# First image of an attention and cluster kernel: the second block's first keys kept in SBUF, its queries taken from SBUF, the maximum spread one value pair sooner

## The chip, the cores and the metric

The kernel runs on one core of a Trainium2 chip. TensorE multiplies matrices (its weight loads are listed apart from its matmuls), VectorE (DVE) and ScalarE (ACT) work on SBUF and PSUM, GpSimd (POOL) works on SBUF, and SyncE (SP) issues most of the DMAs. The metric is the device time of one execution in microseconds, as the median of several runs.

## The reference

Four images of 256 channels and 64 x 64 pixels pass two layers. The first is self-attention over the 4096 pixels of an image:

```python
q = jnp.einsum('oc,bcn->bno', wq, xf) + bq            # 32 channels
k = jnp.einsum('oc,bcn->bon', wk, xf) + bk[None, :, None]
attn = jax.nn.softmax(jnp.einsum('bnd,bdm->bnm', q, k), axis=-1)
v = jnp.einsum('oc,bcn->bon', wv, xf) + bv[None, :, None]
out = jnp.einsum('bcn,bmn->bcm', v, attn).reshape(B, Cc, H, W)
return gamma[0] * out + x
```

The second layer, which the change doesn't touch, is a group norm, a clustering of the pixels, an MLP with GELU, and a pointwise convolution, all over the same images.

## The kernel before, in words

**Tiles and units.** An image's 4096 queries are cut into 8 blocks of 512, and its 4096 keys into 8 groups of 512. A unit is one group against one block, so an image has 64 units, numbered block by block: unit 8 is the second block's first unit and takes key group 0 again. Each unit has two halves of 256 keys. `products` (L484) makes a half's scores in a PSUM tile `sc`, `kept` (L501) copies them on ACT into the unit's slot `s` in SBUF, and `highest_of` (L506) takes the running maximum `top` on DVE. In `half` (L521) the copy comes first and the maximum reads the same PSUM tile after it. The maximum of a block is folded (`fold`, L566), turned over by four transposes (`turned_over`, tile `tt`), reduced and put on a diagonal `dg` (`across`, L578), and spread over all partitions by one matrix product into the PSUM tile `hold` (`spread`, L640). `exps` (L649) subtracts it from the scores on DVE and takes the exponentials on ACT; `factors` (L666) adds pieces on DVE and POOL; `weigh` (L716) multiplies them with the values into the accumulators `av`.

**Keys and queries.** Both have 32 channels, cut into a high and a low part and stacked four times along the partitions, so that one product of 128 partitions multiplies all pairs of parts. `projected` (L346) projects four blocks at a time into 128 partitions; `halves_of` (L359) splits the result. There are two ways to the stacked form. `straight` (L381) moves one block with four DMAs of 64 KB from SBUF to SBUF, one for each part, each from 32 partitions to every fourth partition. Or `written` (L376) first writes the split rows to DRAM with four DMAs of 256 KB (on POOL's queue here), and `q_block` (L458) or `k_unit` (L463) loads a stacked block back with one DMA of 256 KB on SP, which waits for the writes.

**The first image's start** is `alone` (L865), an order written out by hand; the program keeps it on every engine. `staged` (L393) projects blocks 0 to 3 of keys and queries into one tile `st` and makes the stacked keys of groups 0 to 3 and the queries of block 0 straight from it. Groups 4 to 7 are made straight from the tile `hl_k`, with 16 DMAs on SP that are issued after unit 0. While the 8 units of block 0 are scored, the values are projected pair by pair (`v_pair`, L453: eight matmuls, then an eviction on ACT), and POOL writes the split rows to DRAM after units 2 to 5. After unit 3 the queries of block 1 and the keys of unit 8 are loaded back from DRAM; the keys of unit 9 are loaded when unit 8 begins (`begun`, L469). Behind these loads on SP's queue come the weights `mix`, `fvb`, `wproj` and the smaller parameters (`load_rest`, L176). After the last unit come the fold, `v_pair(11)`, the transposes, unit 8's first half, `v_pair(12)`, `across`, `v_pair(13)`, `spread`, `v_pair(14)`, and `wf` (L283: four small matmuls and two copies on ACT); then `exps(0)`.

**Buffers.** Keys in the stacked form for units 0 and 1 and for 8 onward take two buffers (tag `k`) in turn; queries take two (tag `q`). The pool `spool` has 13 buffers of 8 KB a partition, given to tiles as they come: four tiles of the image, `st`, three sums, and the slots of units 0 to 4 fill it. Slots 5 and 6 take the buffers of the first two image tiles. The third and fourth image tiles are still read by `v_pair(8)` to `v_pair(15)`, so the slot of unit 7 takes the buffer of `st`: in the program's memory map, the two have the same address. Its first write, ACT's copy of unit 7's first half, therefore waits for all DMAs that read `st`.

Of the kernel before, what the change touches and what calls it, by code (L numbers as in the profile page):

```python
# [9 lines left out]
F32R = mybir.dt.float32r  # L10
# [4 lines left out]
P = 128  # L15
# [3 lines left out]
NB = 512  # L19
# [10 lines left out]
RG, GRP = 4, N // NB  # L30
# [30 lines left out]
def attention_then_cluster_block(  # L61
# [26 lines left out]
    work = ctx.enter_context(tc.tile_pool(name="work", bufs=2))  # L88
# [87 lines left out]
    def load_rest():  # L176
        load_mix("first")
        yield
        nc.sync.dma_start(out=fvb[:, ED:], in_=v_b.partition_broadcast(P))
        nc.sync.dma_start(out=wproj_s[:ED], in_=wproj)  # L180
        nc.sync.dma_start(out=wproj_s[ED:, :], in_=pc[:, ipb : ipb + 1].rearrange("c o -> o c"))
        yield
        for i, f in enumerate(behind):
            f()
            if i == 2:
                yield
        yield
        nc.gpsimd.tensor_tensor(pw_q[1], pw_q[1], pw_q[3], ALU.add)
        nc.gpsimd.tensor_scalar(pw_q[3], pw_q[3], -1.0, None, ALU.mult)
        yield  # L190
# [63 lines left out]
    def roots():  # L254
        for s, v in ((dw_d, "dw_v"), (pw_s, "pw_v")):
            rsqrt(s, par(v), BN_EPS)
        table(AF.Exp)
# [80 lines left out]
    def attention(b, xs, ys):  # L338
# [5 lines left out]
        qs, ks, slots, mxs, accs, tops, rdens, ts = {}, {}, {}, {}, {}, {}, {}, {}  # L344
# [28 lines left out]
        def part_of(which, c, hi, lo):  # L373
            return (hi if c in ((0, 2) if which == "k" else (0, 1)) else lo).bitcast(F32)
# [6 lines left out]
        def straight(which, r, dst, hi, lo, other=nc.sync):  # L381
            for c in range(4):
                (other if c % 2 else nc.sync).dma_start(
                    out=dst[c::4].bitcast(F32),
                    in_=part_of(which, c, hi, lo)[r * D : (r + 1) * D],
                )

        def stacked(which, nb):

            i, r = divmod(nb, RG)  # L390
            return own[which][i, r * D : (r + 1) * D].rearrange("d c n -> (d c) n")

        def staged():  # L393

            st = spool.tile([P, 4, NB], F32R, tag="s", name=f"st_{b}")
            ps = ps_s.tile([P, 2, NB], F32, tag="s", name=f"pr_{b}")
            k0, q0 = (st[:, 0], st[:, 1]), (st[:, 2], st[:, 3])
            for j, w in enumerate("kq"):  # L400
                projected(w, 0, ps[:, j])
            halves_of("k", *k0, ps[:, 0])
            k_straight(0, k0)
            qs[0] = work.tile([P, NB], F32R, tag="q", name=f"q_{b}_0")
            halves_of("q", *q0, ps[:, 1])
            straight("q", 0, qs[0], *q0, nc.scalar)
            for u in range(1, 4):
                k_straight(u, k0)
            return k0, q0
# [27 lines left out]
        def v_step(i, k):  # L437
            if i == k == 0:
                own["v"] = big.tile([P, N // P, C], F32, tag="v", name=f"v_{b}")
            if i % 2 == k == 0:  # L440
                vps[0] = ps_m.tile([P, 2, C], F32, tag="m", name=f"vp_{b}_{i // 2}")
            o = (i * P) % XT
            nc.tensor.matmul(  # L443
                vps[0][:, i % 2, :],
                xs[i * P // XT][:, k, o : o + P],
                wv_s[:, k, :],
                start=(k == 0),
                stop=(k == KC - 1),
            )
            if i % 2 and k == KC - 1:  # L450
                nc.scalar.copy(own["v"][:, i - 1 : i + 1, :], vps[0])

        def v_pair(i):  # L453
            for j in range(2 * i, 2 * i + 2):
                for k in range(KC):
                    v_step(j, k)

        def q_block(nb):  # L458

            qs[nb] = work.tile([P, NB], F32R, tag="q", name=f"q_{b}_{nb}")  # L460
            nc.sync.dma_start(out=qs[nb].bitcast(F32), in_=stacked("q", nb))

        def k_unit(u):  # L463

            g = u % GRP
            ks[u] = big.tile([P, NB], F32R, tag="k", bufs=2, name=f"k_{b}_{u}")
            nc.sync.dma_start(out=ks[u].bitcast(F32), in_=stacked("k", g))
# [30 lines left out]
        def tiles(t):  # L498
            return t.rearrange("p r (h n) -> p r h n", h=2)

        def kept(u, h, sc):  # L501
            nc.scalar.copy(slots[u][:, PAIR[h]].rearrange("p h r n -> p r h n"), tiles(sc))  # L502
# [69 lines left out]
        def turned_over(nb, tp):  # L572
            top = tops.pop(nb)
            for j in range(4):
                nc.tensor.transpose(tp[:, j, :], top[:, 0, j * P : (j + 1) * P], ident)
            return tp

        def across(nb, tag="w2", tp=None):  # L578
            if tp is None:
                tp = turned_over(nb, ps_m.tile([P, 4, P], F32, tag="m", name=f"tt_{b}_{nb}"))  # L580
            mx = small.tile([P, 4], F32, tag="mx", name=f"mx_{b}_{nb}")
            nc.vector.tensor_reduce(mx, tp, AX.X, ALU.max)
            dg = work.tile([P, 4, P], F32, tag=tag, bufs=1, name=f"dg_{b}_{nb}")
            nc.vector.tensor_tensor(
                dg,
                ident.unsqueeze(1).to_broadcast([P, 4, P]),
                mx.unsqueeze(2).to_broadcast([P, 4, P]),
                ALU.mult,
            )
            return dg  # L590
# [49 lines left out]
        def spread(nb, dg):  # L640


            if nb == 0:
                own["hold"] = ps_s.tile([P, 2, NB], F32, tag="s", name=f"hold_{b}")
            nc.tensor.matmul(
                own["hold"][:, 0], ones, dg.rearrange("p j n -> p (j n)"), start=True, stop=True
            )
# [52 lines left out]
        def sums(g):  # L700


            if "sums" not in own:
                own["sums"] = [
                    spool.tile([P, GRP, 2, P], F32, tag="s", name=f"sum{j}_{b}") for j in range(3)
                ]
            a11, a12, a21, a22 = left(g)
            s2, s3, s4 = (t[:, g] for t in own["sums"])
            return [
                lambda: plus(s3, a21, a11, ALU.subtract),  # L710
                lambda: plus(a21, a22, a21, ALU.subtract),
                lambda: plus(s2, a21, a11),
                lambda: plus(s4, a12, s2, ALU.subtract),
            ]
# [148 lines left out]
        dgs, t31, t4s = {}, {}, {}  # L863

        def alone():  # L865

            roots()
            for i in range(2):
                v_pair(i)
            k0, q0 = staged()  # L870
            for i in range(2, 5):
                v_pair(i)

            def added(*gs):
                for g in gs:
                    for f in sums(g):
                        f()

            added(0, 1)
            rest = load_rest()  # L880
            for u in range(GRP):
                half(u, 0)()
                if u < GRP - 1:
                    half(u, 1)()
                else:

                    sc = products(u, 1)
                    highest_of(0, tiles(sc))
                    kept(u, 1, sc)
                if u == 0:  # L890
                    k1 = halved("k", 1, False)
                    for i in range(4, GRP):
                        k_straight(i, k1)
                elif u == 1:
                    q1 = halved("q", 1, False)
                else:
                    v_pair(u + 3)
                    if u % 2 == 0:
                        added(u // 2 + 1)
                if 1 < u < 6:  # L900
                    written("kqkq"[u - 2], (u - 2) // 2, *(k0, q0, k1, q1)[u - 2], nc.gpsimd)
                if u == 3:
                    q_block(1)
                    k_unit(GRP)
                if 2 < u < 7:
                    next(rest)
            fold(0)
            v_pair(11)
            added(5)
            tp = turned_over(0, ps_m.tile([P, 4, P], F32, tag="m", name=f"tt_{b}_0"))  # L910
            half(GRP, 0)
            v_pair(12)
            dgs["dg"] = across(0, "w2", tp)
            v_pair(13)
            added(6)
            spread(0, dgs["dg"])
            v_pair(14)
            wf()
            exps(0)
            factors(0)  # L920
            v_pair(15)
            half(GRP, 1, True)
            added(7)
            for _ in rest:
                pass
# [1240 lines left out]
```

## Time and profile before

| what | value |
|---|---|
| median of three runs | 3116.73 us (3112.5 to 3117.52) |
| profiled execution, its own time | 3112.69 us |
| its span | 3110.9 us |
| granted TensorE clock | 0.998 |
| TensorE matmuls busy | 3042.2 us, 98% of the span |
| VectorE, GpSimd, ScalarE busy | 80%, 75%, 57% |
| TensorE busy from 45 to 63 us | 14.87 of 18 us |
| TensorE busy from 120 to 400 us | 276.76 of 280 us |

Times within the profile are counted from the start of the span. The stretch that the change touches lies between 28 and 63 us. In a timeline, a line has the start, the duration, the engine, the line of the program, the operation, output and input tiles, their shape, and how many instructions are merged; brackets hold the idle time before it and what ended that. A "q" after an engine's name is its sequencer, which issues DMAs.

### The profile page before, as it was taken

Reading aid. Unit: us, or ns where it says so; the run is one execution under the profiler, and the core shown is the slowest. Engines: PE = TensorE matmul, PEld = TensorE weight load, DVE = VectorE, ACT = ScalarE, POOL = GpSimd, SP = SyncE. Lnnn points to the kernel's source line nnn. Section 1 sums busy time; section 2 is a strip of 40 time slices with the busy share of each in tenths; the row PEclk is TensorE's granted clock in tenths of the full one; section 3 lists DMA queues with packets and bytes.
Section 4 is the critical chain, followed back from the end, with each engine's and each line's share of the span. In section 5 each row is a group of like instructions: output and inputs, shape, how many; then the busy total and the mean of one; then the engine's idle time right before and its main releaser. Section 6 shows DMA issues by size and latency. Waiting matters only on the chain.

```text
span 3110.9 us, 41355 instructions
## 1 busy us (share of the span) xinstructions
PE 3042.2 (98%) x14210; PEld 2488.0 (80%) x14210; DVE 2501.5 (80%) x3548; ACT 1779.4 (57%) x2817; POOL 2327.7 (75%) x2243
## 2 busy tenths in 40 slices
PE   8999999999999999999999999999999999999999
PEld 5788887788688888878868888887877888885886
DVE  4998888777798888877779888877768988887675
ACT  5666664544566666454456666645456666655444
POOL 6888887477588888648758888965766988894563
PEclk9999999999999999999999999999999999999999
DMA  5112226100112113510011222441011212150000
GB/s 175 45 58 65 62 84 176 58 18 28 52 45 68 55 62 108 159 48 28 18 58 45 69 62 65 117 147 35 28 41 48 59 54 68 55 154 2 13 21 28
DMA packets 105570, 200.40 MB, mean 64 GB/s; under 512 B 14880, under 2 KB 30864, under 8 KB 103824
## 3 DMA queue, kind: packets, MB, share of 16 engines
q1 hardware_dynamic: 100464, 178.66, 18.0%
q0 software_dynamic: 4256, 18.90, 2.9%
q8 instruction: 113, 1.85, 0.2%
q14 instruction: 97, 0.79, 0.1%
q10 hardware_dynamic: 640, 0.20, 0.0%
HBM read 147.01 MB, written 48.34 MB: 63 GB/s over the span
## 4 chain that ended last, share of the span: by engine, by line
PE 74%; DVE 9%; POOL 8%; issue 3%; ACT 3%; DMA 2%; SPq 1%; POOLq 0%; ACTq 0%; DVEq 0%
PE av L734 34%; PE mo L1776 10%; PE sc L489 7%; PE hq L1859 5%; PE hp L1859 3%; PE hr L1859 3%; PE fv L1334 3%; POOL acc L664 3%; DVE s L655 2%; POOL t L664 2%; DVE top L513 2%; PE vp L443 1%; POOL s L664 1%; PE mo L1760 1%; DMA w<-in_w 1%
## 5 line engine op out<-in xcount | busy, mean ns | idle before, releaser
L502 ACT COPY s<-sc 128x1024 f32<-128x1024 f32 x512 | 515.1, 1012 | 427.5 <-PE sc L489 419.0
L655 DVE TENSOR_TENSOR s<-s,hold 128x1024 f32<-128x1024 f32 x512 | 598.4, 1209 | 10.7 <-ACT hold L638 5.5
L664 POOL TENSOR_TENSOR acc<-acc,t 128x512 f32<-128x512 f32 x408 | 541.4, 1347 | 0.0
L734 PE MATMUL av<-s,sum 128*128 128x256 f32 x2048 | 526.9, 380 | 3.7 <-POOL s L664 3.5
L734 PE MATMUL av<-t,v 128*128 128x256 f32 x2048 | 527.1, 380 | 2.4 <-POOL t L664 2.2
L734 PE MATMUL av<-s,v 128*128 128x256 f32 x2048 | 525.7, 379 | 2.2 <-ACT xn L1727 1.1
L664 POOL TENSOR_TENSOR s<-t,s 128x512 f32<-128x512 f32 x256 | 340.5, 1330 | 226.3 <-DVE t L678 158.9
L678 DVE TENSOR_TENSOR t<-s,hold 128x1024 f32<-128x1024 f32 x256 | 311.7, 1218 | 189.8 <-POOL acc L664 93.3
L513 DVE TENSOR_TENSOR top<-sc,top 128x1024 f32<-128x1024 f32 x350 | 426.6, 1219 | 21.6 <-ACT s L502 18.0
L734 PEld LDWEIGHTS av<-s,v 128*128 128x128 f32 x2048 | 387.2, 189 | 64.6 <-ACT xn L1727 2.3
L734 PEld LDWEIGHTS av<-t,v 128*128 128x128 f32 x2048 | 387.5, 190 | 63.1 <-POOL t L664 8.4
L734 PEld LDWEIGHTS av<-s,sum 128*128 128x128 f32 x2048 | 387.9, 190 | 61.1 <-POOL s L664 8.6
L1814 ACT ACTIVATE hs<-hs,pv_s 128x256 f32<-128x256 f32 x496 | 232.6, 503 | 352.3 <-DVE hs L1850 352.3
L489 PE MATMUL sc<-q,k 128*128 128x512 f32 x1024 | 391.6, 466 | 22.2 <-ACT s L502 10.5
L1776 PE MATMUL mo<-hs,w 128*128 128x256 f32 x1512 | 384.9, 381 | 0.0
L664 POOL TENSOR_TENSOR t<-s 128x512 f32<-128x512 f32 x256 | 329.8, 1288 | 45.4 <-PE av L734 31.9
L1776 PEld LDWEIGHTS mo<-hs,w 128*128 128x128 f32 x1512 | 283.6, 190 | 47.2 <-ACT hs L1814 6.3
L659 ACT ACTIVATE hold<-s 128x512 f32<-128x512 f32 x256 | 154.2, 602 | 214.4 <-DVE s L655 214.2
L1850 DVE TENSOR_TENSOR hs<-hq,hs 128x256 f32<-128x256 f32 x496 | 198.5, 421 | 85.8 <-PE hq L1859 75.5
L661 ACT ACTIVATE s<-s 128x1024 f32<-128x1024 f32 x256 | 266.9, 1043 | 0.0
L489 PEld LDWEIGHTS sc<-q,k 128*128 128x128 f32 x1024 | 173.7, 189 | 110.9 <-DVE top L513 59.1
L734 PE MATMUL av<-t,sum 128*128 128x256 f32 x1024 | 262.4, 378 | 0.0
(292 smaller groups left out, 4844.2 us busy)
## 6 DMA issues: line engine op xcount, KB each, us to landing
k<-k SPq DMA_DIRECT2D x248, 256.0 KB, 2.7
x<-in_x SPq DMA_DIRECT2D x62, 512.0 KB, 6.8
out<-xn SPq DMA_DIRECT2D x62, 256.0 KB, 2.1
att<-t SPq DMA_DIRECT2D x56, 256.0 KB, 4.0
x<-att POOLq DMA_DIRECT2D x12, 1024.0 KB, 9.7
w<-in_w SPq DMA_DIRECT2D x8, 1024.0 KB, 11.4
q<-q SPq DMA_DIRECT2D x31, 256.0 KB, 4.1
rden<-row_rd SPq DMA_DIRECT2D x28, 256.0 KB, 3.7
```

What stands on the lines that cost most here:

```text
L489: nc.tensor.matmul(sc[:, r, :], k_s[:, (2 * h + r) * P : (2 * h + r + 1) * P], qs[u // GRP], start=True, stop=True,)
L502: nc.scalar.copy(slots[u][:, PAIR[h]].rearrange("p h r n -> p r h n"), tiles(sc))
L513: nc.vector.tensor_tensor(top, src, top if saved[nb] is None else saved[nb], ALU.max)
L655: nc.vector.tensor_tensor(sh, sh, mb.to_broadcast([P, 2, 2, QW]), ALU.subtract)
L661: nc.scalar.activation(s[:, PAIR[1]], s[:, PAIR[1]], AF.Exp)
L664: nc.gpsimd.tensor_tensor(out, x, y, op)
L678: nc.vector.tensor_tensor(t31[u], s[:, B11 : B22 + 1 : 2], b12.to_broadcast([P, 2, 2, QW]), ALU.add)
L734: nc.tensor.matmul(av[bank][:, half_ * QW : (half_ + 1) * QW], a[:, r], t[:, r], start=(g == 0 and r == 0 and i in (1, 7, 2, 4)), stop=(g ...
L1776: return nc.tensor.matmul(bank[:, half * HB : (half + 1) * HB], a[:, j], t, start=start, stop=stop)
L1814: nc.scalar.activation(src, src, AF.Gelu_apprx_tanh, bias=pvc("b1", P, j + 4 * (i > 1)))
L1850: nc.vector.tensor_tensor(dst, ps, term, ALU.add)
L1859: nc.tensor.matmul(out, w, x, start=True, stop=True)
```

## The change

Three things change in `alone`. The stacked keys of groups 0 and 1, which units 0 and 1 use, stay in their two buffers and serve units 8 and 9 too, so that their two loads from DRAM go. The queries of block 1 are made by `straight` from `st`, with four DMAs of 64 KB on SP, issued after unit 2; the load from DRAM after unit 3 goes. The writes to DRAM stay. And `spread` comes before `v_pair(13)` and `added(6)` instead of after them.

```diff
                 if 1 < u < 6:
                     written("kqkq"[u - 2], (u - 2) // 2, *(k0, q0, k1, q1)[u - 2], nc.gpsimd)
-                if u == 3:
-                    q_block(1)
-                    k_unit(GRP)
+                if u == 2:
+
+                    ks[GRP], ks[GRP + 1] = ks[0], ks[1]
+                    qs[1] = work.tile([P, NB], F32R, tag="q", name=f"q_{b}_1")
+                    straight("q", 1, qs[1], *q0)
                 if 2 < u < 7:
                     next(rest)
             fold(0)
...
             half(GRP, 0)
             v_pair(12)
             dgs["dg"] = across(0, "w2", tp)
+            spread(0, dgs["dg"])
             v_pair(13)
             added(6)
-            spread(0, dgs["dg"])
             v_pair(14)
             wf()
             exps(0)
```

## The prediction

> **What bounds the kernel now.** I read the page first. TensorE's matmuls are busy 98% of the span, at a granted clock of 0.998, so a wait of TensorE is time lost unless it is covered. The change touches only the first 63 us, where TensorE is less busy (14.87 of 18 us between 45 and 63 us, by the busy times of stretches). So I looked there at the list of waits and then at the timelines of the engines.
>
> ```profile
> span 3110.9 us, 41355 instructions
> PE 3042.2 (98%) x14210; PEld 2488.0 (80%) x14210; DVE 2501.5 (80%) x3548; ACT 1779.4 (57%) x2817; POOL 2327.7 (75%) x2243
> ```
>
> The waits between 44 and 64 us (total, times, longest): TensorE waits 1.2 us for the keys of unit 8, the wait that the change aims at; ACT's copy into a slot ended one wait on a DMA; and DVE's maximum waits for that copy.
>
> ```profile
> DVE top L513 <- ACT s L502: 2.2, 2, 1.2
> PE sc L489 <- DMA k<-k: 1.2, 1, 1.2
> ACT s L502 <- DMA k<-hl_k: 0.6, 1, 0.6
> ```
>
> The timelines of ACT, DVE and TensorE in that stretch show the chain: unit 7's first copy at 46.20, two maxima from 47.25, the fold and the second copy at 49.83, two evictions of values from 50.74, the transposes at 51.43, unit 8's scores at 53.29, the spread at 57.28, the subtraction at 58.34, the exponentials at 60.94.
>
> ```profile
> 46.20 1.01 ACT L502 COPY s<-sc 128x1024 f32<-128x1024 f32 x1 [0.59 <-DMA k<-hl_k]
> 49.83 1.01 ACT L502 COPY s<-sc 128x1024 f32<-128x1024 f32 x1 [2.62 <-DVE top L513]
> 50.74 1.08 ACT L451 COPY v<-vp 128x512 f32<-128x512 f32 x2
> ...
> 60.81 0.25 ACT L292 COPY fvb<-wf_p 128x96 f32<-128x96 f32 x1
> 60.94 0.62 ACT L659 ACTIVATE hold<-s 128x512 f32<-128x512 f32 x1
> ```
>
> ```profile
> 47.25 2.55 DVE L513 TENSOR_TENSOR top<-sc,top 128x1024 f32<-128x1024 f32 x2 [1.23 <-ACT s L502]
> 52.82 0.69 DVE L584 TENSOR_TENSOR dg<-ident,mx 128x512 f32<-128x512 f32 x1
> 58.34 2.35 DVE L655 TENSOR_TENSOR s<-s,hold 128x1024 f32<-128x1024 f32 x2 [4.82 <-PE hold L645]
> ```
>
> ```profile
> 51.43 0.63 PE L575 MATMUL tt<-ident,top 128*128 128x128 f32 x4 [1.18 <-ACT v L451]
> 53.29 0.70 PE L489 MATMUL sc<-q,k 128*128 128x512 f32 x2 [1.23 <-DMA k<-k]
> 53.83 3.61 PE L443 MATMUL vp<-wv_s,x 128*128 128x256 f32 x16
> 57.28 1.02 PE L645 MATMUL hold<-dg,ones 128*128 128x512 f32 x2
> 59.86 0.38 PE L287 MATMUL wf_p<-ident,mix_first 128*96 128x128 f32 x2
> ```
>
> Last, the straight DMAs on SP (64 KB each), from 28 to 35 us and from 35 to 42 us. Min, median and max of issue time and of time to landing more than double, just when POOL's queue begins to write 256 KB pieces to DRAM (from 34.8 us).
>
> ```profile
> L383 SPq DMA_DIRECT2D k<-hl_k x11: 537/592/594, 28.5 to 34.8; - x11
> DMA to landing us min/median/max: 2.0/2.1/2.9
> ...
> L383 SPq DMA_DIRECT2D k<-hl_k x6: 592/914/1780, 34.8 to 39.8; - x6
> DMA to landing us min/median/max: 2.9/4.7/6.4
> ```
>
> **The change, part by part.**
>
> *Loads removed.* Three loads of 256 KB leave SP. Unit 8's scores then follow the transposes, which end at 52.06 (51.43 + 0.63), instead of the landing of the keys: TensorE gains 53.29 - 52.06 = 1.23 us. The load for unit 9 was issued at 56.01, off any wait. Keeping the keys costs nothing: the next keys to take the first buffer, unit 10's, waited for unit 8's last product before (issued at 63.19, landed 2.6 us later, used at 71.54), and they still do.
>
> *Four DMAs added on SP.* They stand behind the 16 pieces of `k<-hl_k`, the last of which is issued at 39.81 and takes 1.74 us, to 41.55. They wait for nothing. Before, the query load sat on SP until 44.92 for POOL's writes, and `mix` followed at 46.55. Four issues at 0.59 to 1.78 us, with 0.05 between, end between 44.1 and 48.9, so `mix` moves by -2.5 to +2.4 us. `wf` reads it at 59.86, and in the trace its two pieces, issued at 46.55 and 48.11, take 6.7 us in the median to land (to about 55): more than 2.4 us of cover, and two loads less ahead of it. The writes on POOL's queue keep their place, and POOL's own instructions do too.
>
> *A wait that this adds.* The four DMAs read `st`, and unit 7's slot has `st`'s buffer. Its first copy, at 46.20, already waits for POOL's writes out of `st`; now it waits for the four pieces too. Behind it on ACT stand the second copy and the evictions of value pairs 10 and 11, the first of which gives the transposes their PSUM bank. DVE's maximum waits for the copy, the fold for the maximum. TensorE meanwhile has pairs 10 and 11, to 50.25, and then nothing until the transposes. So each microsecond of delay of this copy delays the transposes by one.
>
> When do the pieces land? The last is issued after three others. At the best issue time it starts at 41.6 + 3 x 0.64 = 43.5 and lands 2.9 us later, at 46.4; at the worst it starts at 41.6 + 3 x 1.83 = 47.1 and lands 6.4 later, at 53.5. I take the medians of the rows from 35 to 42 us, since POOL's second eight writes, issued from 42.2 to 46.5, are in flight just as the first eight were: 41.6 + 3 x 0.96 = 44.5, plus 4.7, is 49.2. The copy then starts 49.2 - 46.2 = 3.0 us late (ends: 0.2 and 7.3).
>
> Here the Trainium skill has a price. "DMA: Bandwidth & Descriptors", in "Anatomy of one DMA", fits a DMA of the POOL path alone as about 2.0 us and its bytes at 436 GB/s, which for 64 KB is an estimate of 2.15 us. The quiet rows (2.1) agree; by it the last piece would land at 43.5 + 2.15 = 45.7, nothing would wait, and the sum would be -1.2 us. The same page's "Issuing engines are not separate DMA queues" says that DMAs of all issuing engines interleave on the same 16 DMA engines, which speaks against the change and for the crowded rows (4.7).
>
> *The spread moved.* It now follows pair 12 instead of pair 13, so `hold` is ready 1.73 us sooner within TensorE's order (eight matmuls, half of 3.61, are 1.8). `dg` must be there: it ends 53.51 - 52.06 = 1.45 us after the transposes, and unit 8's scores and pair 12 take 0.54 + 1.73 = 2.3 us, which covers it by 0.8. The subtraction then ends 1.7 us sooner. But the exponentials stand on ACT behind the two copies of `wf`, whose matmuls come after pair 14; the work of TensorE up to there is the same. Before, the last of these copies begins at 60.81 and the first exponential at 60.94, so ACT's order was a bound too, and the subtraction (58.34 + 2.35 = 60.69) was hardly later than that. Gain taken: 0. It can't be over the 1.7 us; a loss has one place, `wf`'s PSUM bank, which needs pair 13's eviction: 1.0 us later in order (the spread's two matmuls), it ends at 59.1 instead of 58.06, still before 59.86. So 0.
>
> *Sum.* -1.2 + 3.0 + 0 = +1.8 us. After 63 us nothing waits for a load (unit 10's keys have 5.7 us of cover), so the shift runs through to the end. The profiled execution took 3112.69 us (span 3110.9, 1.8 around it): it becomes 3114.5. It lies at the lower end of the runs shown; median 3116.73, and the mean of the three runs and the profiled one is 3114.86. On that mean I predict 3116.7.
>
> **The rivals.**
>
> *No wait at all.* The pieces land before 46.2. For it: the 2.1 us of quiet rows, and that SP's last pieces before them are through by 45.4. Against: the crowded rows, whose minimum of 2.9 already gives 46.4. Time: -1.2 us on the mean of 3114.86, 3113.6.
>
> *The spread's gain gets through.* If ACT could start the exponentials 1.7 us sooner, with no added wait, -1.2 - 1.7 = -2.9 us: 3112.0. Against: ACT's order, just shown.
>
> *Slower: the pieces land very late.* One mechanism, at ACT's first copy of unit 7: with issue and landing at their worst rows, it starts at 53.5 and the sum is -1.2 + 7.3 = +6.1 us: 3121. It is slower than before from a landing at 47.4 (46.2 + 1.2) on, and beyond what can be told from no change from 53.6 on. For it: issues of 1.78 and 1.23 us in a row and a landing after 6.4 us do stand in the trace. Against: all worst values at once.
>
> **How the numbers follow.** 0.2% is 6.2 us, about what a measurement of this kernel can tell from no change: below 3110.5 is faster, above 3123.0 slower. Chances: the forecast, a delay of 0.2 to 6 us, 0.66; no wait 0.18; the spread's gain 0.06; very late 0.10. The runs shown scatter by 5 us, more than most of this, so each case is widened by that: the first three end within the bounds but for 0.04 below and 0.02 above; the last is put above. Faster 0.04, same 0.84, slower 0.12. The range goes from the no-wait case on a low run (3112.5 - 1.2, cut to 3112) to the late case on a middle run (3116.7 + 6.1, cut to 3122).
>
> **What would show it.** The first copy of unit 7 waits for `q<-st` and starts near 49.2 instead of 46.20; the transposes near 54.4; unit 8's scores directly behind them with no wait for `k<-k`; `hold` about 2.3 us behind the scores' start; and a subtraction that ends some 1.7 us before the first exponential, which still follows `wf`'s copies. It is wrong if that copy still starts at 46.2, if the exponentials come before 60, or if the time from 63 us to the end differs by more than 3 us from before.

## The result, and the profile after

| | before | changed |
|---|---|---|
| median, 21 runs each | 3114.91 us | 3120.01 us |
| lowest to highest | 3111.38 to 3117.52 us | 3116.45 to 3124.11 us |
| profiled execution | 3112.69 us | 3121.16 us |
| its span | 3110.9 us | 3119.4 us |

The ratio is 1.0018, with a 95% interval of 1.0011 to 1.0024: the change costs 5.6 us (3.4 to 7.5). The medians differ by 5.1 us. The two profiled executions differ by more, 8.5 us, since the one of before lies 2.2 us below its median and the other 1.2 above.

The timelines of ACT, DVE and TensorE in the changed kernel, in the stretch that was shown of before. First ACT: unit 7's first copy, the second copy of `wf`, the first exponential.

```profile
52.87 1.01 ACT L502 COPY s<-sc 128x1024 f32<-128x1024 f32 x1 [7.65 <-DMA mix_first<-in_wfv]
...
68.88 0.25 ACT L292 COPY fvb<-wf_p 128x96 f32<-128x96 f32 x1
69.01 0.62 ACT L659 ACTIVATE hold<-s 128x512 f32<-128x512 f32 x1
```

```profile
53.92 2.55 DVE L513 TENSOR_TENSOR top<-sc,top 128x1024 f32<-128x1024 f32 x2 [8.31 <-ACT s L502]
64.68 2.35 DVE L655 TENSOR_TENSOR s<-s,hold 128x1024 f32<-128x1024 f32 x2 [3.71 <-PE hold L645]
```

```profile
46.23 3.62 PE L443 MATMUL vp<-wv_s,x 128*128 128x256 f32 x16
58.10 1.09 PE L575 MATMUL tt<-ident,top 128*128 128x128 f32 x4 [8.26 <-ACT v L451]
58.84 1.20 PE L489 MATMUL sc<-q,k 128*128 128x512 f32 x2
59.84 3.62 PE L443 MATMUL vp<-wv_s,x 128*128 128x256 f32 x8
63.25 1.40 PE L645 MATMUL hold<-dg,ones 128*128 128x512 f32 x2
```

The wait for keys is gone: unit 8's scores follow the transposes directly. But the copy starts at 52.87 instead of 46.20, and DVE and TensorE stand behind it: TensorE idles 8.26 us ahead of the transposes. The view puts the copy's idle time down to `mix`, which stands next on SP's queue, but the copy doesn't read `mix`, and `mix` lands only after the copy has started: its two pieces, issued at 46.11 and 47.94, take 7.0 and 5.8 us, to 53.1 and 53.8. The four query pieces are what the copy waits for, as the straight DMAs issued on SP between 40 and 46 us show (issue times, then min, median and max of time to landing, which take in one last piece of the keys):

```profile
L383 SPq DMA_DIRECT2D q<-st x4: 806/1122/2054, 40.8 to 45.1; - x4
...
DMA to landing us min/median/max: 4.4/5.4/7.5
```

The last piece is issued at 45.1 and has the longest landing, 7.5 us: it is in at 52.5, and the copy starts 0.3 later.

And there is a second thing: before, eight matmuls of a value pair took 1.73 us from start to start of the next; here, one pair alone takes 3.41 (59.84 to 63.25). The stretches of the changed kernel show why (a row gives the stretch and its length in us; the busy time and instructions of TensorE, its weight loads, DVE, ACT and POOL; then the granted clock, the DMA share and GB/s):

```profile
49.90:53.70 3.80, 0.00 (x0) 0.00 (x0) 0.00 (x0) 0.83 (x1) 0.00 (x0) 1.00 0.82 197
53.80:58.00 4.20, 0.00 (x0) 0.00 (x0) 3.14 (x3) 1.58 (x4) 0.00 (x0) 0.50 0.46 90
58.00:64.00 6.00, 5.90 (x15) 4.60 (x16) 1.71 (x2) 2.02 (x4) 3.23 (x4) 0.50 0.01 3
64.00:70.00 6.00, 5.74 (x28) 4.68 (x27) 2.35 (x2) 2.53 (x7) 2.90 (x4) 1.00 0.00 0
```

TensorE had nothing to do from 49.85 on. Its clock fell to 0.50 about 4 us later and stayed there for the first 6 us of work after the idle time. In the kernel before it is 1.00 in all of these stretches.

So at the first exponential the changed kernel is 69.01 - 60.94 = 8.07 us late. The account: the copy 52.87 - 46.20 = +6.67; from the copy to the transposes 5.23 in both; from the transposes to unit 8's scores 0.74 instead of 1.86, which is the 1.23 won less 0.11 of slow clock; from the scores to `hold` 4.41 for the scores and one pair, where 2.27 would do at the full clock (0.54 and 1.73 in the trace of before), +2.14; `hold` 1.23 instead of 0.86, +0.37. Together 6.67 - 1.23 + 0.11 + 2.14 + 0.37 = 8.06, of which 2.6 us are the slow clock.

### The profile page after: what moved, and what is told of

It reads as the page before. It is cut to its first block, busy times and chain, and to the rows that moved or that the text cites. A ratio compares the mean times of both kernels' runs of the same rounds, so it can differ in the third digit from the quotient of the medians.

```text
span 3119.4 us, 41354 instructions
## 1 busy us (share of the span) xinstructions
PE 3043.9 (98%) x14210; PEld 2494.4 (80%) x14210; DVE 2504.6 (80%) x3548; ACT 1779.3 (57%) x2817; POOL 2327.8 (75%) x2243
## 4 chain that ended last, share of the span: by engine, by line
PE 74%; DVE 10%; POOL 8%; ACT 3%; issue 3%; DMA 2%; SPq 1%; ACTq 0%; POOLq 0%; DVEq 0%
PE av L734 34%; PE mo L1778 10%; PE sc L489 7%; PE hq L1861 5%; PE hr L1861 3%; PE hp L1861 3%; PE fv L1336 3%; POOL acc L664 2%; DVE top L513 2%; DVE s L655 2%; PE vp L443 2%; POOL t L664 1%; PE mo L1762 1%; DMA w<-in_w 1%; POOL s L664 1%
```

## The experiments

The theory after the result has two parts: the four DMAs out of `st` hold unit 7's first copy, since its slot has the buffer of `st`, and the idle time that this gives TensorE lets its clock fall. The rivals are that another part of the change costs the time, that the traffic and not the buffer does, and that the clock is a side effect without a price.

### One part of the change alone

The queries from SBUF alone, with the keys loaded as before and the spread where it was:

```diff
-                if u == 3:
-                    q_block(1)
+                if u == 2:
+                    qs[1] = work.tile([P, NB], F32R, tag="q", name=f"q_{b}_1")
+                    straight("q", 1, qs[1], *q0)
+                if u == 3:
                     k_unit(GRP)
```

> The kernel before with the queries of block 1 alone taken from SBUF; the keys of unit 8 are still loaded, the spread stays. My theory (the whole loss comes from the four DMAs that read the staging tile, since unit 7's slot has its buffer): unit 7's first copy starts near 52.9 instead of 46.2, the TensorE clock is at half from about 58 to 64 us, and the time is 5 us more than before or a little over, as with the whole change. The rival (kept keys or the spread bring the loss): within 1 us of before.

Median 3120.74 us against 3113.89, ratio 1.0024 (1.0015 to 1.0033): the whole loss is there. The copy, on ACT's timeline, and the clock:

```profile
52.95 1.01 ACT L502 COPY s<-sc 128x1024 f32<-128x1024 f32 x1 [7.62 <-DMA mix_first<-in_wfv]
...
67.51 0.62 ACT L659 ACTIVATE hold<-s 128x512 f32<-128x512 f32 x1
```

```profile
54.10:60.80 6.70, 2.61 (x9) 2.27 (x10) 4.50 (x5) 2.63 (x4) 2.40 (x4) 0.50 0.47 107
60.90:66.00 5.10, 5.10 (x23) 4.11 (x22) 1.24 (x2) 1.45 (x3) 2.60 (x4) 1.00 0.00 0
```

The first exponential is 6.57 us later than before. The half clock ended at 60.9 here and at 64 in the changed kernel, so its price is not the same in each execution.

The keys alone:

```diff
                     q_block(1)
-                    k_unit(GRP)
+                    ks[GRP], ks[GRP + 1] = ks[0], ks[1]
```

> The kernel before with the keys of units 8 and 9 kept in SBUF, and nothing else; the queries of block 1 still come from DRAM. My theory: the wait of 1.23 us for unit 8's keys goes, the scores follow the transposes at 52.1, unit 7's first copy stays at 46.2, and the time is 1.2 us less than before. The rival (the queries' landing or something else is late in their place): no gain, within 0.3 us of before.

Median 3114.74 against 3113.89, ratio 1.0000 (0.9991 to 1.0009). On the trace the mechanism is as expected: the scores of unit 8 start at 52.76, directly behind transposes at 52.37. But in this execution the transposes themselves were 0.94 later than in the profiled execution of before, and 1.2 us is inside the interval of 2.8 either way. The runs neither show the gain nor exclude it.

The spread alone:

```diff
+            spread(0, dgs["dg"])
             v_pair(13)
             added(6)
-            spread(0, dgs["dg"])
             v_pair(14)
```

> The kernel before with the spread alone moved ahead of the 13th value pair. My theory (the exponentials stand on ACT behind the two copies of wf): hold is ready 1.7 us sooner and the subtraction ends sooner, the first exponential starts within 0.3 us of 60.94, and the time is that of before within 1 us. The rival (the spread's gain gets through): the exponentials start at 59.2 and the time is 1.7 us less.

Median 3113.35 against 3113.89, ratio 0.9999 (0.9990 to 1.0008). TensorE's line of the spread and ACT's lines after it:

```profile
55.78 1.02 PE L645 MATMUL hold<-dg,ones 128*128 128x512 f32 x2
```

```profile
61.04 0.25 ACT L292 COPY fvb<-wf_p 128x96 f32<-128x96 f32 x1
61.17 0.62 ACT L659 ACTIVATE hold<-s 128x512 f32<-128x512 f32 x1
```

`hold` comes 1.5 us sooner (55.78 against 57.28; 1.73 counted from unit 8's scores), and the first exponential doesn't: it follows `wf`'s copy by 0.13, as before.

### The buffer

The staging tile in the buffer that slot 10 takes at about 70 us, in the changed kernel and, as a control, in the kernel before. Unit 7's slot then has the buffer of the second image tile.

```diff
-            st = spool.tile([P, 4, NB], F32R, tag="s", name=f"st_{b}")
+            st = swap.tile([P, 4, NB], F32R, tag="w1", name=f"st_{b}")
```

> The changed kernel with the staging tile in the buffer that slot 10 takes later, so that unit 7's slot gets the buffer of the second image tile and its first copy waits for none of the DMAs out of the staging tile. My theory (the shared buffer is the cause): the copy starts at about 45 to 46.2 us, the transposes near 51.4, no half clock, unit 8's scores at 52.1 to 52.9 when the last piece of the queries lands, and the time is 0.4 to 1.2 us less than before. The rival (the traffic of the four pieces, not the buffer, makes the loss): still 4 us or more over before.

> The kernel before with the staging tile in the buffer that slot 10 takes later, as a control for that move. My theory: in the kernel before the copy waited for its scores and not for the writes out of the staging tile, so nothing changes: within 0.5 us of before. The rival (the writes out of the staging tile held something in the kernel before): a gain of over 0.5 us.

The changed kernel with this move: 3114.10 against 3114.50, ratio 0.9997 (0.9988 to 1.0006). The control: 3114.95, 1.0004 (0.9995 to 1.0012). The loss is gone with the shared buffer, with the same DMAs in flight, and the move by itself does nothing that these runs can tell. TensorE's timeline of the changed kernel with the move, at unit 8's scores:

```profile
54.27 0.70 PE L489 MATMUL sc<-q,k 128*128 128x512 f32 x2 [1.38 <-DMA q<-st]
```

The copy starts at 47.03. The scores of unit 8 now wait 1.38 us for the query pieces, which are in at 54: the wait for keys of before, 1.23, has only changed its name. So the trace shows no gain, and the runs (3.7 us less to 1.9 more than before) can't tell the expected 0.4 to 1.2.

### Why the pieces land late

POOL's second eight writes, out of `hl_k` and `hl_q`, two units later:

```diff
-                if 1 < u < 6:
-                    written("kqkq"[u - 2], (u - 2) // 2, *(k0, q0, k1, q1)[u - 2], nc.gpsimd)
+                if u in (2, 3, 6, 7):
+                    i = u - 2 if u < 4 else u - 4
+                    written("kqkq"[i], i // 2, *(k0, q0, k1, q1)[i], nc.gpsimd)
```

> The changed kernel with GpSimd's second eight writes to DRAM, out of the second staging tiles, issued after units 6 and 7 instead of 4 and 5. If the four query pieces land late because those writes crowd the DMA engines from 42 us on: they land by 46.5 to 48 us, unit 7's first copy starts there, there is no half clock, and the time is within 1 us of before. If SP's own issue makes them late: the last piece still lands near 52.5 and the time stays 5 us over before.

Median 3115.06 against 3114.50, ratio 0.9999 (0.9991 to 1.0008). The straight DMAs of this kernel, issued from 43 to 47 us (the last row takes in one piece of the keys, the 4.9):

```profile
L383 SPq DMA_DIRECT2D q<-st x4: 592/596/1725, 43.2 to 46.2; - x4
...
DMA to landing us min/median/max: 2.1/2.1/4.9
```

Without the second eight writes in flight, the last three pieces take 0.6 us to issue again and 2.1 to land; the first, at 43.2, still took 1.7 and 3.5. The last piece is issued later than in the changed kernel (46.2 against 45.1) and lands 4.2 us sooner, at 48.3; the copy starts at 48.67, 0.7 us later than expected, and the clock stays at 1.00. So it is the writes that hold the pieces up, in both issue and landing.

### The clock

The changed kernel again, and beside it the changed kernel with matmuls that fill TensorE's idle time; first with 18 of them, then with 14:

```diff
+            warm = ps_a.tile([P, NB], F32, tag="a0", name="warm")
+            for _ in range(14):
+                nc.tensor.matmul(
+                    warm[:, :C], wv_s[:, 0, :P], wv_s[:, 1, :], start=True, stop=True
+                )
             tp = turned_over(0, ps_m.tile([P, 4, P], F32, tag="m", name=f"tt_{b}_0"))
```

> The changed kernel with 18 matmuls of 128x128 by 256 (about 0.43 us each, 7.8 us together) on TensorE between the 11th value pair and the transposes; their result is not used. Theory of two parts (6.7 us of late copy, less 1.2 us of key wait, plus 2.6 us because the granted clock fell to 0.50 in the idle time): the clock stays at 1.00, unit 8's scores to the spread take 2.3 us again instead of 4.4, and the time is 2.6 us less than the changed kernel's, some 2.5 us over before. Theory of one part (the late copy alone makes the loss): the time stays at 5 us over before.

> The changed kernel itself once more, beside the next one on the same chip. Both theories: 5 to 6 us more than before. In its profiled execution unit 7's first copy starts at about 52.9; whether the clock falls to 0.50 near 54 to 64 us in every execution is open, since the idle time of TensorE there is 8.3 us in each.

> The changed kernel with 14 matmuls of 128x128 by 256 (6.0 us) between the 11th value pair and the transposes instead of 18, which had ended after the transposes could start (58.65 against 57.9). If the half clock takes its 2.6 us in most executions, this is 2 to 3 us less than the changed kernel beside it. If the half clock comes and goes, or is paid back later, the two are within 1 us.

With 18 matmuls: 3120.67 against 3113.89, ratio 1.0020 (1.0012 to 1.0029), 6.2 us over before (3.7 to 9.0) where 2.5 were expected. So this kernel is not faster than the changed one, and the expectation missed. Two things in its trace are part of that: the matmuls ran to 58.65 and held the transposes back themselves, by 0.8 us, and though its clock stays at 1.00 up to the first exponential, which comes at 66.67 instead of 69.01, the rest of the kernel takes 1.9 us longer in this execution (3052.2 against 3050.4), with 23.4 us of half clock far from the change against 12.7 (last section).

With 14: 3119.23 against 3114.07, ratio 1.0015 (1.0006 to 1.0024). The changed kernel beside it: 3120.89, 1.0020 (1.0011 to 1.0029). The changed kernel's stretches in this second execution and its transposes and `hold` on TensorE, then the same with 14 matmuls:

```profile
55.30:62.00 6.70, 3.03 (x10) 2.60 (x11) 4.33 (x5) 3.00 (x4) 2.82 (x4) 0.50 0.27 53
62.20:68.00 5.80, 5.80 (x27) 4.57 (x26) 2.35 (x2) 1.53 (x3) 2.23 (x4) 1.00 0.00 0
```

```profile
58.97 1.08 PE L575 MATMUL tt<-ident,top 128*128 128x128 f32 x4 [8.36 <-ACT v L451]
...
63.12 1.02 PE L645 MATMUL hold<-dg,ones 128*128 128x512 f32 x2
```

```profile
52.00:58.00 6.00, 5.06 (x24) 4.12 (x22) 3.14 (x3) 2.56 (x4) 0.00 (x0) 1.00 0.66 133
58.00:60.00 2.00, 1.95 (x11) 1.79 (x12) 1.25 (x2) 1.26 (x2) 1.81 (x3) 1.00 0.01 2
```

```profile
58.05 0.63 PE L575 MATMUL tt<-ident,top 128*128 128x128 f32 x4 [0.99 <-ACT v L451]
...
60.71 1.02 PE L645 MATMUL hold<-dg,ones 128*128 128x512 f32 x2
```

That an idle TensorE lets its clock fall is shown: filled, it stays at 1.00. From the transposes to `hold` it is then 2.66 us (58.05 to 60.71) instead of 5.15 in the first execution of the changed kernel and 4.15 (58.97 to 63.12) in the second. So the fall costs 1.5 us in the second execution and 2.9 in the first, with 0.37 of `hold` itself. (The account above has 2.6 for the first, since it lets unit 8's scores follow the transposes after 0.63 us; with 14 matmuls they follow after 0.39.)

Over all runs the medians are 1.7 us apart, the way that was expected, but less than 2 to 3, and the intervals overlap. The price of the clock is read from the traces; the runs with 14 matmuls agree with it but don't prove it, and those with 18 don't show it. What they do show is that most of the loss stays without the slow clock: 4.7 us (1.9 to 7.5) with 14 matmuls. At the first exponential 66.09 - 60.94 = 5.15 us are left, which is the late copy (52.82, +6.62) less the key wait (1.23), to within 0.3.

### Getting the gain

With the buffer moved, `wf` behind the last value pair:

```diff
             v_pair(14)
-            wf()
             exps(0)
             factors(0)
             v_pair(15)
+            wf()
```

> As the kernel with the staging tile in slot 10's buffer, and wf moved from ahead of the first exponentials to behind the last value pair. My theory (ACT's order held the spread's gain back): the first exponential starts about 1.7 us sooner against the scores of unit 8 than before, GpSimd's chain of sums after it starts sooner too, and the time is 1.5 to 3 us less than before. The rival (TensorE's order bounds this stretch anyway): no more than the 0.4 to 1.2 us without this move.

Median 3113.20 against 3114.50, ratio 0.9997 (0.9989 to 1.0006): nothing that can be told. ACT's timeline says why the expectation missed:

```profile
59.72 0.59 ACT L451 COPY v<-vp 128x512 f32<-128x512 f32 x1 [1.14 <-PE vp L443]
60.20 0.61 ACT L659 ACTIVATE hold<-s 128x512 f32<-128x512 f32 x1
```

With `wf`'s copies out of the way, the eviction of pair 14 stands in front of the exponentials. They start 7.25 us behind unit 8's scores, where it was 7.65 before.

So the last two kernels put all of this together: the buffer moved and the writes late, and, in the second, the exponentials ahead of pair 14 as well.

```diff
             v_pair(13)
             added(6)
-            v_pair(14)
-            wf()
             exps(0)
+            v_pair(14)
             factors(0)
             v_pair(15)
+            wf()
```

> The changed kernel with the staging tile in slot 10's buffer and GpSimd's second eight writes after units 6 and 7, but with the exponentials and wf where they are in the changed kernel. My theory: unit 7's first copy at 46.2 to 46.5, unit 8's scores at 51.9 to 52.2 with no wait for keys or queries, the first exponential 7.6 us behind these scores (as before), so at 59.5 to 59.8, and the time 1.2 us less than before. Then the exponentials' move is worth 2 us of the 4 us that the kernel with all three moves gained. The rival (the late writes or the tile's place bring the gain by themselves): 3 us or more less than before.

> The changed kernel with three moves: the staging tile in slot 10's buffer, GpSimd's second eight writes after units 6 and 7, and the first exponentials ahead of pair 14 with wf behind the last pair. My theory: unit 7's first copy at about 46.2, unit 8's scores at 52 with no wait, the first exponential at about 57.8, 3 us sooner than before; the time 2 to 3 us less than before, if GpSimd's sums, which are busy without a break from 64 to 91 us in the kernel before, are what carries the start on. The rival (TensorE's own order carries it on): 1.2 us less, the wait for the keys alone.

Without the exponentials' move: 3112.59 against 3114.00, ratio 0.9994 (0.9985 to 1.0003), which is -1.9 us and agrees with 1.2, though the interval takes in no change. The copy starts at 45.63, unit 8's scores at 51.25 with no wait, the first exponential at 58.90. With it: 3110.07 against 3114.07, ratio 0.9987 (0.9978 to 0.9996): 4.0 us less (1.2 to 6.9), faster than both kernels. Its copy starts at 46.17, as before. ACT's timeline of that kernel, at the first exponential and at the one of five units later, and the latter in the kernel before:

```profile
57.61 0.60 ACT L659 ACTIVATE hold<-s 128x512 f32<-128x512 f32 x1
...
87.54 0.60 ACT L659 ACTIVATE hold<-s 128x512 f32<-128x512 f32 x1 [0.51 <-DVE s L655]
```

```profile
90.86 0.60 ACT L659 ACTIVATE hold<-s 128x512 f32<-128x512 f32 x1 [0.52 <-DVE s L655]
```

In the kernel before, these exponentials start at 60.94 and 90.86. The 3.33 us won at the first are 3.32 at the later one, though TensorE's first weighing came only 1.8 us sooner (61.19 against 63.00). GpSimd's sums keep the lead too: the first starts at 61.04 instead of 64.38, one of five units later at 86.72 instead of 90.04, and GpSimd is busy without a break between. So the start is carried on through GpSimd's sums, as expected, and not through TensorE's order. How the 4 us divide between the moves is not settled by the runs: the two kernels' intervals overlap.

## Why the prediction was right or wrong

*The loads removed* (-1.23 us): right. The scores follow the transposes without a wait, in the changed kernel and with the keys alone.

*The wait added* (+3.0): here the prediction failed, in the size. The place was right, and the chain behind it too: the copy waits for the query pieces, ACT, DVE and TensorE stand behind it, and moving the buffer takes the loss away. The step that failed is "44.5, plus 4.7, is 49.2. The copy then starts 49.2 - 46.2 = 3.0 us late": the copy started 6.67 us late. The last piece was issued at 45.1 and not at 44.5, it landed after 7.5 us and not 4.7, and the copy followed 0.3 us behind that. The 4.7 was a median over six pieces, the first three of which were issued as POOL's writes began and landed after 2.9, 3.4 and 3.7 us, the later three after 6.3, 6.4 and 5.6. The four query pieces were all issued with the writes already in flight and took 5.2, 4.4, 6.2 and 7.5; for the last of them the longest row, 6.4, was the nearer one. I had used it for the worst case alone. (Of these rows the prediction also says that all of min, median and max more than double. That holds for the longest issue and for the median and the longest landing; the median issue goes from 592 to 914 ns, the shortest landing from 2.0 to 2.9 us.) With this one term at its measured size the sum is -1.2 + 6.7 = +5.5 us.

*The spread* (0): right. Alone it makes `hold` 1.5 us sooner and the exponentials no sooner. What I named in front of them, `wf`'s copies, was only the first of two: the eviction of pair 14 stands there too.

*A term put at nothing.* "Each microsecond of delay of this copy delays the transposes by one" held: 5.23 us lie between the two in both kernels. But the sum carries the delay on from there with the work after the transposes at the durations of before, without a reason. TensorE came out of 8 us of idle time at a granted clock of 0.50, and that costs 1.5 to 2.9 us in the traces. The page of before shows a clock of 0.998 for the whole, and the stretches I read were too long to show a lower one, though the kernel before has them too (0.53 from 2870 to 2877 us). The Trainium skill has the rule, which I hadn't weighed: "TensorE: Matmul & The Clock Gate", Part 1, says that TensorE goes to half rate after an idle window of about 3.4 us and returns after a busy one, with windows that run freely. For this stall the traces agree: the clock fell 3.9 and 4.7 us after the work ended in the two executions of the changed kernel, and the half-clock stretches seen here last about 6.8 us (54.1 to 60.9 and 55.3 to 62.1) and 10.2 us (53.8 to 64.0), two and three times 3.4. Elsewhere 2.0 us of idle time was enough (last section), and there the measurement decides.

*The sum.* -1.2 + 3.0 + 0 = +1.8 us was predicted. At the first exponential the parts as measured are -1.2 + 6.7 + 0 and 2.6 for the clock, 8.1 us, in the first execution of the changed kernel, and -1.2 + 7.5 + 0 and 1.3 for the clock (counted as in the account after the result), 7.6, in the second. The runs give 5.6 (3.4 to 7.5) and, measured again, 6.2 (3.4 to 9.0), so both profiled executions lie above the middle, and how much of the 5.6 is the clock is not known from the runs. The forecast was a change too small to be told; the measured one is three times as large, and its whole interval lies above no change. My bound of 6.2 us for what can be told was also too wide for 21 runs, which tell 2 us apart.

*The rivals.* No wait at all: no; even with the later writes moved away, the last piece lands at 48.3, behind the 46.2 of before. The spread's gain: no, and the reason held. Very late pieces: that was close to what happened, at 52.9 of the 53.5 that its worst rows gave. I had called it all worst values at once; two of them, the issue and the landing behind the writes, come together, since both went away with the writes. That its +6.1 us is so near the measured 5.6 is in part luck, since it has no term for the clock either.

## What to carry to other kernels

A transfer made straight from a staging tile is a new reader of that tile: look up which tile takes its buffer next, and price the wait at the landing time of a piece in the same depth of queue, not at the median of a stretch in which the queue fills. A wait that leaves TensorE idle can cost more than its length, since the work behind it may start at half clock: after 8 us of idle time it did here in all three profiled executions that had it, after 2.0 us in 4 of 14. And before moving one step ahead, list everything that stands in front of its consumer on the consumer's own engine: here two things did, and only when both had moved did the gain come through.

## What the runs showed of the hardware that I had not expected

The half clock comes elsewhere too, and not in the same places in each execution. Later in the kernel, a gap of 2.03 us on TensorE (scores that wait for the maximum) ends at 229.49 in the profiled execution of before and at 237.93 in that of the changed kernel. Before, the clock stays at 1.00 behind it; in the changed kernel it falls:

```profile
230.00:238.00 8.00, 7.97 (x37) 6.61 (x37) 6.54 (x7) 5.07 (x7) 5.75 (x5) 1.00 0.58 166
```

```profile
238.10:241.40 3.30, 3.30 (x8) 2.56 (x9) 3.30 (x4) 1.81 (x3) 3.23 (x3) 0.50 0.26 85
```

There, 8 matmuls run in 3.3 us where 16 do at the full clock, so one such stretch costs some 1.7 us. The second execution of the changed kernel has one of 6.8 us from 601.4, the one with 18 matmuls one of 6.8 us from 1367.0. The same instructions with the same gap meet the clock's fall in one execution and not in the next.

The traces show what decides it. In each of the 14 profiled executions, all steps of the clock lie on a grid of 3.41 us that begins at its first rise; in the changed kernel 9.38, then 53.75, which is 13 grid steps later, 63.99, 238.07 and 241.48. The gap at this place is 2.02 to 2.05 us long in all 14. In four of them it lies whole within one grid step (in the changed kernel 235.91 to 237.93, within 234.66 to 238.07; the others are the keys alone, the late writes alone, and the late writes with the buffer moved), and in these four and no others the clock falls at the end of that step. In the other ten the gap is split between two steps, with at most 1.87 us in one, and the clock stays at 1.00. Over the whole of the 14 traces, counting TensorE's idle time in each grid step that began at the full clock: all 35 steps with over 1.95 us were followed by half clock, and of some 12,600 steps with less only 8 were, 6 of them with 1.91 or 1.92; the other two are those before the stretches from 601.4 and 1367.0, with 1.44 and 1.36, which this doesn't explain. Where the grid lies against the kernel differs from execution to execution, by the start of the first rise (9.4 to 12.9 us).

These stray stretches may be a good part of the 6 to 8 us by which the 21 runs of each of the two kernels scatter: of those of the changed kernel, the six with a mean clock of 0.998 take 3118.6 us on average and the five with 0.996 take 3121.3. In the 14 profiled executions, over all kernels, the time from the first exponential to the end goes from 3049.1 us, with 9.3 us of half clock in it, to 3053.5, with 24.0. That is a correlation; no run here takes the stray stretches away.
